# An FNO tokenizer with a transformer layer on one core: other matrix products and another order of steps in passes two and three

## The chip, the cores and the metric

The kernel runs on one core of a Trainium2 chip. The core has a matrix engine (TensorE, PE in the profile; its weight loads are listed apart as PEld), a vector engine (DVE), a scalar engine (ACT), a general engine (POOL) and a queue engine (SP) that here does nothing but issue transfers. All transfers share the core's 16 DMA engines. The metric is the device time of one execution in microseconds.

## The reference, cut to what matters

A batch of 64 images of 256 x 256 points goes through four Fourier layers of 32 channels, whose result is joined with 77 rows of text per image and goes through one transformer layer (attention, then a feed-forward over a selected half of the tokens). The change lies in the Fourier layers:

```python
v = h @ p_w + p_b                                  # (B, 32, 256, 256)
for i in range(4):
    x_ft = rfft2(v)                                # only 24 x 12 modes are used
    out_ft = modes of x_ft times fw1[i], fw2[i]    # mixes the 32 channels
    v = irfft2(out_ft) + einsum('bcxy,cd->bdxy', v, w_w[i]) + w_b[i]
    v = (v - mean(v)) * rsqrt(var(v) + 1e-5) * bn_g[i] + bn_b[i]   # over batch and points
    if i < 3: v = relu(v)
out = einsum('bcxy,cu->bxyu', v, q_w) + q_b
```

The mean and variance of layer i+1 are taken over all images, so a whole pass over the batch must be done before the next layer can be normalised. For the variance the kernel needs, among other sums, the sum over all points of the square of `v @ w_w[i+1]`.

## The kernel before, in words

**Stages.** `forward_first` transforms the raw images (0 to 110 us). Then, for each layer, `mix` multiplies the modes by the layer's weights and works out the normalisation; and for layers 0, 1 and 2 `layer` makes one pass over the 64 images. These are the three passes. The first (about 190 to 2547 us) takes the raw image as its input; the second (2624 to 5560 us) and the third (5637 to 8530 us) load the image's values that the pass before has stored in DRAM. The transformer layer follows (8640 us to the end).

**One image in a pass** is cut into eight chunks t = 0 to 7 of 1 MB each: 128 partitions (four groups of 32 channels) by 8 rows of 256 values. All data is fp32; every matrix product is issued as two MATMULs. The steps of one image, as `layer` names them:

- `am` loads the image's modes into `ams` (two transfers on SP, then a scaling on POOL). `sp0`, `sp1` expand the modes along x for chunks 0 to 3 and 4 to 7 (L662, PE), and `spT0`, `spT1` turn the result around on DVE into `y0`, `y1` (L670).
- `ld` t loads a chunk of the layer's input into `vin` (L656, two transfers of 512 KB on SP). The first pass has none.
- `pre` t makes the layer's output for a chunk in PSUM: 8 products of the inverse transform along y (L682) and 16 products of the channel matrix on 32x32 tiles (L693). `evA` and `evB` apply the ReLU to the two halves and write them to `vo`, on ACT (`.a`, L705) or DVE (`.d`, L707), as the word says.
- `st` t stores the chunk for the next pass (L714, two transfers of 512 KB).
- `turn` t transposes 32x32 blocks of the chunk into `t32` on DVE (L719).
- `prod` t multiplies the chunk by the next layer's channel matrix, 16 products on 32x32 tiles (L730), and `sqA`, `sqB` square and sum the two halves on ACT (L741).
- `y0` to `y7` transform the whole image along y, 16 products each, all accumulating in the same PSUM tiles (L752); `half`, `zt0` and `zt1` take the result out (L762 on ACT, L770 on DVE).
- `x` transforms along x: for each of three groups of modes four products with the image as the stationary operand (128x128) and 96 columns of the table `FX` as the moving one (L786). `xo` copies the result out on ACT (L797) and `xs` sends it to DRAM (L803).

**What sets the order.** The order is written out by hand: a pass repeats the list of words of `ORDER` once per image (the first entry for the first pass, the second for the second and third). `word@k` does the step for the image k further on, so several images are under way at once. Each engine takes its steps strictly in this order; steps on different engines meet only through semaphores. SP, too, issues transfers in the order of the list, and a transfer that waits holds up those behind it. In the program each transfer on SP also waits for the one eight before it to have landed.

**Buffers.** PSUM is a ring of four tiles of two banks (`take` gives a step the tiles that were freed first, `close` frees one); `pre`, `prod` and `y` take two, `sp` and `x` one. The y steps hold two tiles from y0 until `half` and `zt0`. `vin` and `vo` have four buffers each, `t32` six (a buffer holds two chunks). A `vo` buffer is free again when its chunk has been stored, turned and multiplied. Which chunk follows which in a buffer comes from the order in which they become free: in the second and third pass evA3 and evB3 write the buffer that the latest st6 stores, evA0 that of st5, evA7 that of st4, evA1 that of st2.

Of the kernel before, what the change touches and what calls it, by code (L numbers as in the profile page):

```python
# [9 lines left out]
F32 = mybir.dt.float32  # L10
# [7 lines left out]
C = 32  # L18
M = 12
KX = 2 * M  # L20
# [14 lines left out]
def _tables():  # L35
# [92 lines left out]
ORDER = [(  # L128
# [7 lines left out]
), (  # L136
# [7 lines left out]
)]  # L144

_TABLES, _GRIDS = _tables()
# [7 lines left out]
def tile_fno_fusion_transformer(ctx: ExitStack, tc: tile.TileContext, a, cst_d, grid_d, out):  # L154
    nc = tc.nc
    x = a["x"].rearrange("b x y o -> b x (y o)")
# [3 lines left out]
    const = ctx.enter_context(tc.tile_pool(name="const", bufs=1))  # L160
# [15 lines left out]
    T4, ID, ONES, CHAN = tab("t4"), tab("ident"), tab("ones"), tab("chan")  # L176

    CROW = tab("crow").rearrange("p (n k) -> p n k", n=4)

    epsc = const.tile([128, 1], F32, name="epsc")  # L180
    nc.vector.memset(epsc, EPS)

# [29 lines left out]
    w4 = [w4all[:, i, :] for i in range(L)]  # L212
# [333 lines left out]
    def layer(i, st, src, dst, acc):  # L546
# [3 lines left out]
        EX, FX = EXL[lay], FXL[lay]  # L550
# [3 lines left out]
        with ExitStack() as cx:  # L554
            def pool(name, bufs, **kw):
# [3 lines left out]
            op, yp, cp, xp, zp, tp = (  # L559
                pool(n, k, reuse_waits="tile")  # L560
                for n, k in (("lo", 4), ("ly", 1), ("lc", 1), ("lx", 2), ("lz", 1), ("lt", 6))
            )
# [20 lines left out]
            for n in range(nr):  # L583
# [4 lines left out]
                if n:  # L588
                    nc.vector.tensor_add(a0, a0, a1)
            nc.vector.tensor_copy(ams[1], ams[0])  # L590
            ws = cp.tile([128, C], F32, name="ws")
            if i:
                nc.vector.tensor_mul(ws, w4[i], s_)
            if i == 0:
                mv = [ip.tile([128, 4, 4 * S + 8], F32, name="mv") for n in range(2)]
                mv = [t[:, :, 0:4 * S].rearrange("p q (s y) -> p q s y", s=4) for t in mv]
                for t in mv:
                    nc.sync.dma_start(t, grid_d.rearrange("p (q s y) -> p q s y", q=4, s=4))

            ring, free, clock = {}, [0] * 4, [0]  # L600

            def take(key, n):

                clock[0] += 1
                mine = sorted((k for k in range(4) if free[k] >= 0), key=lambda k: free[k])[:n]
                for k in mine:
                    free[k] = -1
                ring[key] = [(k, pp.tile([128, 2, 512], F32, name=f"ring{k}")) for k in mine]
                return [t for _, t in ring[key]]

            def banks(key):
                return [t[:, n] for _, t in ring[key] for n in range(2)]
# [6 lines left out]
            y_, t32, vin, vo, half_, zts = {}, {}, {}, {}, {}, {}  # L619
# [104 lines left out]
            def prod(b, t, e):  # L724
                take(("prod", b, t), 2)
                ps = banks(("prod", b, t))
                for k in range(4):
                    for n in range(4):
                        j = (n + k) % 4
                        nc.tensor.matmul(  # L730
                            ps[n][32 * j:32 * j + 32], lhsT=w4[i + 1][32 * n:32 * n + 32],
                            rhs=vo[b, t][32 * n:32 * n + 32, 2 * j:2 * j + 2, :], start=True, stop=True,
                            skip_group_check=True, tile_position=(32 * n, 32 * j),
                        )

            def sq(n):
                def run(b, t, e):
                    key = "prod", b, t
                    at = 2 * (8 * b + t) + n
                    ps = ring[key][n][1]  # L740
                    nc.scalar.activation(ps, ps, AF.Square, accum_out=acc[:, at:at + 1])  # L741
                    close(key, n)
                return run
# [21 lines left out]
            def zt(h):  # L765
                def run(b, n, e):
                    if b not in zts:
                        zts[b] = zp.tile([128, 2, 32, C], F32, name="zt")
                    whole = h == 0 or b not in half_
                    nc.vector.transpose(  # L770
                        zts[b][:, h].rearrange("p k c -> p c k"),
                        (ring["y", b][h][1] if whole else half_[b]).rearrange("p n (s c) -> p c (n s)", c=C),
                    )
                    if whole:
                        close(("y", b), h)
                return run

            def x_(b, n, e):
                zt_ = zts.pop(b)
                ps = take(("x", b), 1)[0]  # L780
                for g in range(3):
                    n = 0
                    for h in range(2):
                        for r in range(2):
                            k0 = M * r + 4 * g
                            nc.tensor.matmul(  # L786
                                ps[:, 0, 96 * g:96 * g + 96],
                                lhsT=zt_[:, h, k0:k0 + 4, :].rearrange("p k c -> p (k c)"),
                                rhs=FX[:, h, 48 * r:48 * r + 96], start=n == 0, stop=n == 3,
                            )  # L790
                            n += 1

            xos = {}

            def xo(b, n, e):
                xos[b] = xp.tile([128, 3, 2 * KX], F32, name="xo")
                nc.scalar.copy(  # L797
                    xos[b], ring["x", b][0][1][:, 0, 0:288].rearrange("p (g k) -> p g k", g=3)[:, :, 0:2 * KX]
                )
                close(("x", b), 0)  # L800

            def xs(b, n, e):
# [1 line left out]

            run = dict(
                am=am, lx=lx, ld=ld, sp=sp, spT=spT, pre=pre, evA=ev(0), evB=ev(1), st=st_, turn=turn,
                prod=prod, sqA=sq(0), sqB=sq(1), y=y, half=half, zt0=zt(0), zt1=zt(1), x=x_, xo=xo, xs=xs,
            )
            steps = []
            for word in ORDER[min(i, 1)].split():  # L810
                word, _, late = word.partition("@")
                word, _, e = word.partition(".")
# [100 lines left out]
    with tc.tile_pool(name="tw", bufs=1) as tp, tc.tile_pool(name="tq", bufs=2, space=PSUM) as tq:  # L913
# [5 lines left out]
        for dh in range(2):  # L919
            ps = tq.tile([128, D], F32, name="wtp")  # L920
# [313 lines left out]
```

## Time and profile before

| | |
|---|---|
| median of 5 runs | 11277.61 us (11274.02 to 11296.37) |
| the profiled execution | 11296.37 us, span 11294.6 us |
| mean granted clock of TensorE | 0.984 of full speed |
| second pass, 2624 to 5560 us | PE busy 2796.64, DVE 2182.48, ACT 1747.69 us; DMA share 0.98 |
| third pass, 5637 to 8530 us | PE busy 2759.01, DVE 2159.55, ACT 1729.01 us; DMA share 0.98 |
| transfers of chunks (all three passes) | 3072 stores and 2048 loads of 512 KB |
| median time from issue to landing, 2700 to 5500 us | stores 8.8 us, loads 9.1 us |

The profile lists instructions by source line (L693 is line 693 of the kernel before), with what is written and read by the program's names. A group's row gives the number of instructions, the busy time, the mean duration and the idle time of the engine before them with what ended it. Matmuls overlap and their ends are modelled, so that a busy PE need not be a full PE. The DMA share is the time of all packets over 16 engines; since packets overlap a little, it can read over 1. The profiled execution was the slowest of the five.

### The profile page before, as it was taken

To read this page: it belongs to the slowest core of one execution; us is meant where nothing else is said; L and a number is where in the kernel's file an instruction comes from. 1 tells how busy PE (TensorE), PEld (TensorE's weight loads), DVE (VectorE), ACT (ScalarE), POOL (GpSimd) and SP (SyncE) were. 2 spreads that over 40 slices of the span, in tenths; PEclk is the share of its full clock that TensorE was granted. 3 is DMA by queue.
4 is the path that set the end of the run, shared out by engine and by line. 5 is a ranking of instruction groups with operands and counts; after the bars stand their busy time and mean duration, and the time that the engine had idled before them with its cause. 6 is when DMAs were issued, how large, how long until landed. Compare 5 with 4: busy or idle time off the path is not lost.

```text
span 11294.6 us, 409300 instructions
## 1 busy us (share of the span) xinstructions
PE 10611.1 (94%) x182550; PEld 5729.7 (51%) x182550; DVE 8448.3 (75%) x10381; ACT 6472.7 (57%) x10673; POOL 1446.2 (13%) x2179
## 2 busy tenths in 40 slices
PE   6999999998999999999799999999996999999999
PEld 3555555554444444444444444444443666666666
DVE  6888888887777777777677777777775766666665
ACT  5777777775566655666565666556563333333333
POOL 1111111110000000000000000000000333333333
PEclk8999999998999999999899999999998999999999
DMA  6766676678999999999899999999998555555553
GB/s 212 248 246 247 249 247 247 245 254 316 382 381 383 380 377 377 375 379 378 303 378 381 377 377 380 380 373 377 372 378 296 226 227 227 226 227 227 226 227 138
DMA packets 972545, 3457.31 MB, mean 306 GB/s; under 512 B 149784, under 2 KB 199320, under 8 KB 903832
## 3 DMA queue, kind: packets, MB, share of 16 engines
q1 hardware_dynamic: 905344, 3366.80, 77.8%
q0 software_dynamic: 58288, 60.60, 2.3%
q8 instruction: 1429, 23.41, 0.8%
q10 hardware_dynamic: 7144, 3.72, 0.1%
q14 instruction: 340, 2.79, 0.1%
HBM read 1733.60 MB, written 1696.92 MB: 304 GB/s over the span
## 4 chain that ended last, share of the span: by engine, by line
PE 61%; DMA 21%; DVE 9%; ACT 3%; issue 3%; SPq 2%; POOL 0%; ACTq 0%; DVEq 0%; POOLq 0%
PE ring L752 15%; DMA v<-vo 12%; PE ring L682 9%; PE ring L730 8%; DMA vin<-v 6%; PE ring L693 5%; PE hp L982 3%; PE ring L662 3%; PE pp L1145 3%; PE pp L1156 3%; PE ring L786 2%; DVE vo L707 2%; PE pp L1110 2%; DMA xh<-xo 2%; PE pp L1175 2%
## 5 line engine op out<-in xcount | busy, mean ns | idle before, releaser
L741 ACT ACTIVATE ring<-ring 128x1024 f32<-128x1024 f32 x3072 | 3115.8, 1014 | 1184.3 <-PE ring L730 1121.3
L719 DVE STREAM_TRANSPOSE t<-vo 128x2048 f32<-128x2048 f32 x1536 | 3465.7, 2286 | 21.4 <-DVE vo L707 0.9
L730 PE MATMUL ring<-vo,w 32*32 32x512 f32 x49152 | 2408.1, 600 | 85.0 <-ACT vo L705 69.0
L707 DVE TENSOR_SCALAR vo<-ring 128x1024 f32<-128x1024 f32 x1280 | 1544.7, 1221 | 1192.8 <-PE ring L693 799.1
L705 ACT ACTIVATE vo<-ring 128x1024 f32<-128x1024 f32 x1792 | 1792.3, 1023 | 1038.3 <-PE ring L693 484.7
L752 PE MATMUL ring<-t,cst 32*32 32x512 f32 x49152 | 2075.0, 599 | 53.8 <-issue 47.8
L752 PEld LDWEIGHTS ring<-t,cst 32*32 32x32 f32 x49152 | 909.7, 103 | 935.8 <-issue 635.6
L730 PEld LDWEIGHTS ring<-vo,w 32*32 32x32 f32 x49152 | 802.8, 103 | 1072.0 <-issue 401.5
L682 PE MATMUL ring<-cst,y 24*128 24x256 f32 x16384 | 1229.1, 402 | 77.6 <-DVE vo L707 60.1
L631 POOL TENSOR_TENSOR ams<-ams,bns 48x512 f32<-48x512 f32 x384 | 401.0, 1044 | 6991.5 <-DMA ams<-mix 6720.7
L693 PE MATMUL ring<-vin,ws 32*32 32x512 f32 x32768 | 1276.9, 603 | 18.0 <-issue 13.1
L682 PEld LDWEIGHTS ring<-cst,y 24*128 24x128 f32 x16384 | 789.3, 185 | 991.1 <-DVE vo L707 390.3
L670 DVE STREAM_TRANSPOSE y<-ring 128x1024 f32<-128x1024 f32 x384 | 763.3, 1988 | 329.4 <-PE ring L662 328.3
L682 PE MATMUL ring<-mv,y 29*128 29x256 f32 x8192 | 703.2, 404 | 36.5 <-ACT ring L741 20.1
L682 PEld LDWEIGHTS ring<-mv,y 29*128 29x128 f32 x8192 | 455.2, 185 | 368.9 <-ACT ring L741 210.3
L786 PEld LDWEIGHTS ring<-cst,zt 128*128 128x128 f32 x4608 | 531.9, 192 | 177.2 <-ACT vo L705 114.5
L762 ACT COPY half<-ring 128x1024 f32<-128x1024 f32 x192 | 194.4, 1013 | 737.9 <-PE ring L752 737.8
L1183 POOL DMA_DIRECT2D out_dram<-o x1024 | 510.7, 507 | 661.2 <-DVE o L1178 618.1
L741 ACT ACTIVATION_READ_ACCUMULATOR ring<-ring 128x1 f32 x3072 | 585.3, 191 | 0.0
L786 PE MATMUL ring<-cst,zt 128*128 128x96 f32 x4608 | 563.8, 279 | 6.3 <-DVE zt L770 5.3
L770 DVE STREAM_TRANSPOSE zt<-ring 128x1024 f32<-128x1024 f32 x192 | 377.4, 1965 | 249.7 <-PE ring L752 249.7
L662 PE MATMUL ring<-ams,cst 49*128 49x512 f32 (+1 forms) x1536 | 450.7, 642 | 105.2 <-POOL ams L631 36.7
(374 smaller groups left out, 9757.9 us busy)
## 6 DMA issues: line engine op xcount, KB each, us to landing
v<-vo SPq DMA_DIRECT2D x3072, 512.0 KB, 7.9
vin<-v SPq DMA_DIRECT2D x2048, 512.0 KB, 9.0
ch<-v SPq DMA_DIRECT2D x512, 1024.0 KB, 12.5
mix<-ob SPq DMA_DIRECT2D x96, 512.0 KB, 5.8
ams<-mix SPq DMA_DIRECT2D x384, 96.0 KB, 7.9
xin<-in_x_dram SPq DMA_DIRECT2D x16, 1024.0 KB, 6.0
mv<-in_x_dram POOLq DMA_DIRECT2D x256, 64.0 KB, 7.5
out_dram<-o POOLq DMA_DIRECT2D x1024, 16.0 KB, 3.0
```

The costliest lines, as they stand in the source:

```text
L662: nc.tensor.matmul(ps[:, n, :], lhsT=EX[hv, 128 * h:128 * h + 128], rhs=ams[b % 2][hv], start=True, stop=True, skip_group_check=True,)
L670: nc.vector.transpose(y_[b, h].rearrange("p q c -> p c q"), ring[key][0][1].rearrange("p n (c k) -> p (n c) k", k=32),)
L682: nc.tensor.matmul(ps[n][:, 256 * r:256 * r + 256], lhsT=y_[b, t // 4][32 * n:32 * n + K, q:q + 4, :].rearrange("p q c -> p (q c)"), rhs=m ...
L693: nc.tensor.matmul(ps[n][32 * j:32 * j + 32], lhsT=ws[32 * n:32 * n + 32], rhs=v[32 * n:32 * n + 32, 2 * j:2 * j + 2, :], start=False, sto ...
L705: nc.scalar.activation(to, ring[key][h][1], AF.Relu)
L707: nc.vector.tensor_scalar(to, ring[key][h][1], 0.0, None, ALU.max)
L719: nc.vector.transpose(t32[b, t // 2][:, :, 8 * (t % 2):8 * (t % 2) + 8, :].rearrange("p y s c -> p s y c"), vo[b, t].rearrange("p s (y l) ...
L730: nc.tensor.matmul(ps[n][32 * j:32 * j + 32], lhsT=w4[i + 1][32 * n:32 * n + 32], rhs=vo[b, t][32 * n:32 * n + 32, 2 * j:2 * j + 2, :], st ...
L741: nc.scalar.activation(ps, ps, AF.Square, accum_out=acc[:, at:at + 1])
L752: nc.tensor.matmul(ps[n][32 * j:32 * j + 32], lhsT=FYT[32 * n:32 * n + 32, k, :], rhs=t32[b, j][32 * n:32 * n + 32, k].rearrange("p s c -> ...
L786: nc.tensor.matmul(ps[:, 0, 96 * g:96 * g + 96], lhsT=zt_[:, h, k0:k0 + 4, :].rearrange("p k c -> p (k c)"), rhs=FX[:, h, 48 * r:48 * r + ...
L1183: nc.gpsimd.dma_start(out[b, 64 * n + 16 * g:64 * n + 16 * g + 16].rearrange("(p t) d -> p t d", t=2), o[32 * g + 8 * n:32 * g + 8 * n + 8 ...
```

## The change

Line numbers of the changed kernel are some 9 to 40 higher. Three things change in the second and third pass, and nothing in the first pass's order:

- **x transform.** The stationary operand is now the table: for each of two parts r and two halves h of the image's lines one product of 64 table columns (128x64) with 384 columns of the image as the moving operand, the two halves writing different halves of the partitions. The result lies the other way round, so `xe` copies it to SBUF (here on DVE) and `xt` makes three products with it as the stationary operand (128x128) and a doubled identity `ID2` of 48 columns as the moving one, which adds the two halves and turns them. These are seven products instead of twelve, and two new steps. `xo` reads the other bank.
- **Products for the squares.** For the words `prod1.w` and `prod7.w` the 16 products on 32x32 tiles become 8 products on 64x64 tiles, with the channel matrix twice on the diagonal of a 64x64 matrix (`w64`, made once per pass).
- **Order.** The second list of `ORDER` is another one. Among other things pre6 now stands between y1 and y2, pre2 of the image two further on stands after prod7 at the end, and st7, st0 and st6 of their images are issued among the y steps. The buffers follow each other differently too: evA7 and evB7 now write the buffer that st4 stores, evA0 that of st2, evA1 that of st5, evA6 that of st3, evA4 that of st1, evA5 that of st7, evA3 that of st6 and evA2 that of st0.

```diff
@@ ORDER, second list
-    "pre5 sqB7@-1 zt1@-1 sqA7@-1 pre6 evA5.a ld2@1 st4 evB5.d st5 turn4 evA6.a prod5 x@-1 "
-    "evB6.a sqB5 prod6 sqA5 xo@-1 turn5 pre2@1 sqA6 turn6 sqB6 prod4 evA2.a@1 evB2.d@1 "
-    "sqB4 ld0@1 ld7 sqA4 pre0@1 evB0.d@1 ld3@1 prod2@1 st6 evA0.a@1 turn2@1 sqB2@1 sqA2@1 "
-    "pre3@1 ld1@1 evA3.a@1 st2@1 evB3.d@1 pre7 evB7.d prod3@1 ld5@1 evA7.a sqA3@1 turn7 "
-    "pre1@1 st0@1 am@2 sqB3@1 prod0@1 evA1.a@1 evB1.d@1 sqA0@1 st7 sp1@1 st1@1 ld4@1 y0 "
-    "spT1@1 y1 ld6@1 turn0@1 turn3@1 xs@-2 y2 sqB0@1 prod1@1 y3 sqB1@1 sp0@2 y4 sqA1@1 "
-    "spT0@2 y5 y6 st3@1 turn1@1 y7 half.a pre4@1 zt0 prod7 evB4.d@1 evA4.a@1 "
+    "evB2.a@1 ld5 ld7 pre4 ld0@1 turn6 evA2.a@1 prod6 evA4.a x@-1 evB4.d xe.d@-1 turn4 "
+    "sqB6 prod4 xt@-1 st2@1 sqA6 turn2@1 sqA4 pre5 xo@-1 sqB4 am@2 evA5.d evB5.a pre3@1 "
+    "prod2@1 evA3.d@1 turn5 evB3.a@1 st4 xs@-1 sqA2@1 pre7 sqB2@1 evA7.a prod5 evB7.d "
+    "sqB5 pre0@1 st5 ld1@1 sqA5 prod3@1 turn7 evB0.a@1 sp1@1 sqA3@1 evA0.d@1 pre1@1 "
+    "sqB3@1 spT1@1 evA1.a@1 prod0@1 sqA0@1 ld6@1 evB1.d@1 ld2@2 st3@1 sp0@2 spT0@2 y0 "
+    "ld4@1 y1 st1@1 sqB0@1 turn3@1 turn0@1 pre6@1 y2 y3 evA6.a@1 y4 evB6.a@1 prod1.w@1 "
+    "sqB1@1 st7 sqA1@1 y5 st0@1 y6 st6@1 turn1@1 y7 prod7.w half.a zt0 sqA7 sqB7 ld3@2 "
+    "zt1 pre2@2 "
...
+    ID2 = const.tile([128, 2 * KX], F32, name="id2")
+    nc.vector.tensor_add(ID2, ID[:, 0:2 * KX], ID[:, 64:64 + 2 * KX])
...
+            w64 = cp.tile([128, 2, C], F32, name="w64")
+            nc.vector.memset(w64, 0.0)
+            for n in range(4):
+                nc.vector.tensor_copy(w64[32 * n:32 * n + 32, n % 2, :], w4[i + 1][32 * n:32 * n + 32])
+            w64 = w64.rearrange("p n o -> p (n o)")
...
@@ def prod(b, t, e)
+                if e == "w":
+                    for j in range(4):
+                        for n in range(2):
+                            m = (n + j) % 2
+                            nc.tensor.matmul(
+                                ps[j][64 * m:64 * m + 64], lhsT=w64[64 * n:64 * n + 64],
+                                rhs=vo[b, t][64 * n:64 * n + 64, 2 * j:2 * j + 2, :], start=True, stop=True,
+                                skip_group_check=True,
+                            )
+                    return
...
@@ def x_(b, n, e)
+                if turned:
+                    for r in range(2):
+                        for h in range(2):
+                            nc.tensor.matmul(
+                                ps[64 * h:64 * h + 64, 0, 0:384], lhsT=FX[:, h, 48 * r:48 * r + 64],
+                                rhs=zt_[:, h, M * r:M * r + M, :].rearrange("p k c -> p (k c)"),
+                                start=r == 0, stop=r == 1, skip_group_check=True,
+                            )
+                    return
...
+            def xe(b, n, e):
+                xes[b] = xp.tile([128, 384], F32, name="xe")
...
+                    nc.vector.tensor_copy(xes[b], ring["x", b][0][1][:, 0, 0:384])
+
+            def xt(b, n, e):
+                xe_ = xes.pop(b)
+                for g in range(3):
+                    nc.tensor.matmul(
+                        ring["x", b][0][1][:, 1, 96 * g:96 * g + 2 * KX],
+                        lhsT=xe_[:, 128 * g:128 * g + 128], rhs=ID2, start=True, stop=True,
+                    )
```

More of the change, by code (lines that the diff above doesn't have):

```diff
@@ L598, in layer @@
                     nc.sync.dma_start(t, grid_d.rearrange("p (q s y) -> p q s y", q=4, s=4))
+            turned = "xt" in ORDER[min(i, 1)]
             ring, free, clock = {}, [0] * 4, [0]
@@ L791, in x_ @@
                             n += 1
-            xos = {}
+            xos, xes = {}, {}
+            def xe(b, n, e):
+                xes[b] = xp.tile([128, 384], F32, name="xe")
+                if e == "a":
+                    nc.scalar.copy(xes[b], ring["x", b][0][1][:, 0, 0:384])
+                else:
+                    nc.vector.tensor_copy(xes[b], ring["x", b][0][1][:, 0, 0:384])
[6 more added lines that the diff above has]
+                    )
             def xo(b, n, e):
@@ L797, in xo @@
                 nc.scalar.copy(
-                    xos[b], ring["x", b][0][1][:, 0, 0:288].rearrange("p (g k) -> p g k", g=3)[:, :, 0:2 * KX]
+                    xos[b], ring["x", b][0][1][:, int(turned), 0:288].rearrange("p (g k) -> p g k", g=3)[:, :, 0:2 * KX]
                 )
@@ L806, in layer @@
                 am=am, lx=lx, ld=ld, sp=sp, spT=spT, pre=pre, evA=ev(0), evB=ev(1), st=st_, turn=turn,
-                prod=prod, sqA=sq(0), sqB=sq(1), y=y, half=half, zt0=zt(0), zt1=zt(1), x=x_, xo=xo, xs=xs,
+                prod=prod, sqA=sq(0), sqB=sq(1), y=y, half=half, zt0=zt(0), zt1=zt(1), x=x_, xe=xe,
+                xt=xt, xo=xo, xs=xs,
             )
```

## The prediction

> **What bounds the kernel now.** I read the page first (which stages are long and what is full in them), then the two passes that the change touches as windows, then the list of waits inside one of them, then one image instruction by instruction.
>
> The page's slices show the change's ground: the second and third passes are the two long stretches at 375 to 383 GB/s, with a DMA share of 9 tenths throughout, while PE reads 9 tenths everywhere.
>
> ```profile
> span 11294.6 us, 409300 instructions
> PE 10611.1 (94%) x182550; PEld 5729.7 (51%) x182550; DVE 8448.3 (75%) x10381; ACT 6472.7 (57%) x10673; POOL 1446.2 (13%) x2179
> DMA  6766676678999999999899999999998555555553
> ```
>
> The two passes as windows (columns: length, then busy time of PE, PEld, DVE, ACT, POOL, granted clock, DMA share, GB/s):
>
> ```profile
> 2624.00:5560.00 2936.00, 2796.64 (x59411) 1325.44 (x59420) 2182.48 (x1221) 1747.69 (x2752) 138.31 (x137) 0.99 0.98 376
> 5637.00:8530.00 2893.00, 2759.01 (x58643) 1296.64 (x58645) 2159.55 (x1205) 1729.01 (x2723) 133.81 (x128) 0.99 0.98 377
> ```
>
> Two resources look full, PE at 95% and DMA at 98%. Neither really is: of PE's busy time much is modelled tails, and DMA has dry spots. One image takes 45.4 us (2936/64 is 45.9, with the pass's two ends). Shorter windows inside one image:
>
> ```profile
> 4018.00:4020.00 2.00, 2.00 (x65) 0.85 (x67) 2.00 (x2) 0.79 (x2) 0.00 (x0) 1.00 0.75 297
> 4044.00:4058.00 14.00, 13.19 (x322) 6.52 (x307) 11.01 (x6) 3.64 (x7) 2.09 (x2) 1.00 1.03 413
> 4060.00:4062.00 2.00, 1.74 (x44) 1.04 (x48) 2.00 (x2) 1.89 (x4) 0.00 (x0) 1.00 0.80 317
> 4064.00:4066.00 2.00, 2.00 (x64) 0.60 (x32) 2.00 (x2) 1.07 (x2) 0.00 (x0) 1.00 0.69 270
> ```
>
> A full DMA reads 1.02 to 1.03, and once per image, just after the eight y steps, it falls to 0.7 or 0.8. So DMA alone would allow 45.4 x 0.98/1.02 = 43.6 us an image. SP's queue shows why it runs dry:
>
> ```profile
> 4007.37 1.52 SPq L656 DMA_DIRECT2D vin<-v  x2
> 4014.76 5.29 SPq L714 DMA_DIRECT2D v<-vo  x4
> ...
> 4023.72 1.07 SPq L714 DMA_DIRECT2D v<-vo  x2
> ```
>
> From 4008.9 to 4014.8 SP issues nothing: st4 waits for the evictions of pre4, which PE only reaches after y7. The bill comes twelve microseconds later, in the waits of 2700 to 5500 us (62 images):
>
> ```profile
> ACT vo L705 <- DMA v<-vo: 135.8, 92, 3.4
> DVE vo L707 <- DMA v<-vo: 132.8, 93, 3.4
> ```
>
> Both engines stand still together, 135.8/62 = 2.2 us an image, before evA3 and evB3: their vo buffer is still being stored by st6, which SP issued at 4023.72, late, and which frees them only at 4036.15 (row below), 12.4 us on. That is the one DMA wait of size.
>
> Last, the rows for the new operations, of the image at 4000 us and of the first transform at 40 us:
>
> ```profile
> 4020.72 2.92 PE L786 MATMUL ring<-cst,zt 128*128 128x96 f32 x24
> 4023.57 1.14 PE L730 MATMUL ring<-vo,w 32*32 32x512 f32 x32
> 4036.15 1.94 ACT L705 ACTIVATE vo<-ring 128x1024 f32<-128x1024 f32 x2 [1.99 <-DMA v<-vo]
> ```
> ```profile
> 45.11 1.94 PE L239 MATMUL ups<-xin,cst 128*64 128x512 f32 x8
> ```
>
> Every product is two MATMULs. x takes 4023.57 - 4020.72 = 2.85 us. L730's 32 MATMULs hold 16 tiles at once and stream in two rounds of 0.43 us. L239, on 128*64 tiles, holds two tiles: its 8 MATMULs are four rounds, (1.94 - 0.64)/3 = 0.43 us apart.
>
> **The change, part by part** (128 images in two passes; all else stands).
>
> *x transform.* Out: 24 MATMULs, 2.85 us. In: 8 MATMULs of L239's shape with 384 columns instead of 512, four rounds of 0.43 x 384/512 = 0.32, 1.3 us; then 6 of L786's pitch (2.85/24 = 0.12), 0.7 us; and two entries into another tile shape at some 0.2 (PE's step from L693 to L730, same shape, starts 0.3 after the last MATMUL; into L682 it takes 0.5). Sum 2.4 us: -0.45. Bounds: -1.3 (both parts fully hidden behind prod4's stream) and +0.5 (the 8 not paired: 2.6 + 0.7). The copy xe is 384 columns on DVE: between L797's 0.28 (144 columns) and L707's 1.22 (1024), I take 0.55. It waits for x, and behind it on DVE stand turn4, turn2 and evA5.d; prod2 waits for evA5. That is in the walk below.
>
> *Two products on 64x64 tiles.* 16 MATMULs, four tiles at once, four rounds of 0.43: 1.7 us against 0.86. With the shape changes I take 1.9 against 0.95, twice: +1.9 us an image, all in or right after the y stretch, where PE is alone on the path. Bounds for one: -0.45 (16 MATMULs at L457's 25 ns, 128 in 3.2 us) and +2.6 (the 16 one after the other at 0.21, 3.4 us). I take the value between, since L239's rounds fit it. The Trainium skill (TensorEngine Tiling, Gotcha 1: PSUM Pressure) says that different row tiles cannot use one PSUM bank at the same time; every tiled product in this trace gives each row group its own bank, while the new one lets both row groups write the same bank in different halves. If that made them take turns, the sum would be by the upper bound, +5.1 us an image; no row here shows it.
>
> *Order.* I walk through one image from the end of y7 with PE's prices (pre 1.97, prod 0.95, y 1.1, sp 1.07), ACT 1.02 an eviction and 1.2 a square, DVE 1.22, 2.0 (spT, zt) and 2.28 (turn), 0.25 from one engine to the next, ring tiles and no DMA wait.
> Before: pre4 0, prod7 2.5 (zt0), pre5 3.7, pre6 5.9 (sqA7), prod5 7.9, x 9.4, prod6 12.2, pre2 13.3, prod4 15.9 (sqB6), pre0 17.0, prod2 19.6, pre3 20.7, pre7 23.2, prod3 25.1, pre1 26.7, prod0 28.9, sp1 30.0, y0 31.4, prod1 34.7, sp0 37.2, end of y7 42.7. The image takes 45.4; the 2.7 left over are the 2.2 of DMA wait and 0.5 of small stalls.
> After: prod7.w 0, pre2 2.5 (zt0), pre4 4.5, prod6 6.9 (evA2), x 8.0, prod4 9.5, xt 10.6, pre5 11.4, pre3 13.6, prod2 16.3 (evA5.d behind turn4 and turn2), pre7 17.5, prod5 20.0 (sqB2), pre0 21.2, prod3 23.7 (sqA5), sp1 24.8, pre1 26.2 (sqA3), prod0 28.3, sp0 29.7, y0 30.9, pre6 33.3 (spT0), y2 35.2, prod1.w 38.5, y5 40.4, end of y7 43.7.
> So the engines' own chain grows by 1.0: -0.45 and +1.9 from the two edits, -0.45 from fewer ring waits.
>
> *Transfers in the new order.* A load or store of one chunk is 2.65 us of full DMA. What SP is given now: ld7 4.5, ld0 6.5, st2 6.8, (am) st4 8.2, (xs) st5 16.3, ld1 and ld6 16.3, ld2 and st3 19.5, ld4 23.2, st1, st7, st0 29.7, st6, ld3, ld5 37.5, then ld7 again. st7 and st0 are held back until the y stretch, so the longest pause (29.7 to 37.5) is met with three stores just queued. With a backlog of 2.5 us before st6 the DMA never runs dry; up to some 5 us, every buffer is back in time. The tightest pair is st4 and evA7, which takes its buffer: 8.2 to 19.9, 11.7 us. The same count for the old order wants at least 4.4 us for no dry spot and at most 5 for st6 to land before evA3 (10.2 to 23): no room with SP's issues of 0.4 to 0.8 us each, and the trace has both the dry spot and the wait. So I let 1.8 of the 2.2 us go, and 0.4 stay, at st4 or ld1. Bounds: all 2.2 stays, or all goes.
>
> *Once a pass:* w64's memset and four copies on DVE, 0.2 to 0.4 us each (L590's copy of 512 columns: 0.43), 2 us a pass at most, before a start that waits for the first ams anyway. The new order leads by the same two images; I put the ends at 0, within 10 us.
>
> Sum per image: +1.0 - 1.8 = -0.8 us; 128 x 0.8 = 102 us. Against the profiled execution (11296.37, span 11294.6 and 1.8 around it): 11194. That execution was the slowest of the five, 19 above the median 11277.61; for a median: **11176 us**, 0.9% faster.
>
> **Rivals.**
> *PE becomes the bound and the waits stay (slower).* The y stretch grows to y0 30.9 through prod7.w 45.6 with a pre inside; if st4 lands late before evA7, the wait has only moved. It costs +1.0 with the 2.2 kept: +128 us, 11405. It decides once more than 1.2 of the 2.2 us stay. For it: PE has 95%, and both full resources leave little room (43.7 walked, 43.6 DMA). Against: the list of pauses above.
> *The sixteen MATMULs go one after the other (slower by far):* +5.1 - 1.9 - 0.8 = +2.4 us, 11585.
> *DMA is the only bound:* PE's extra 1.9 us hides in stalls (PE shows 46 us of idle "issue" in 62 images, and the new form issues half the MATMULs), and the image falls to 43.6: -1.8 x 128 = -230, 11048.
> *No change:* the wait and the added PE time cancel, 11278 within 0.2% (23 us, about what a measurement of this kernel can tell).
>
> **How the numbers follow.** Forecast (20 to 190 us less) 0.44; DMA the only bound 0.14; no change 0.08; PE bound with the waits kept 0.28; one after the other 0.06. Faster 0.58, same 0.08, slower 0.34. The likeliest case's own range is 11090 to 11255. For 8 in 10 it must reach nearly to the DMA floor (11048) and to the kept waits (11405): 11060 to 11405, which leaves out the serial case and the far ends.
>
> **What would show it.** Right: waits of ACT and DVE for v<-vo under 0.6 us an image, no 2 us stretch under 0.85 DMA share, x's eight MATMULs 1.3 us, prod.w's sixteen 1.7 us, an image at 44.6. Wrong: evA7 or pre1's products idle on a transfer for 2 us; sixteen MATMULs over 3 us; DVE's evA5 idle-free behind turn2 with prod2 waiting more than 1 us; PE idle at pre6 for spT0.

## The result, and the profile after

The changed kernel takes 11291.62 us (median of 25 runs, 11271.85 to 11301.82) against 11285.33 us of the kernel before (45 runs): a ratio of 1.0005, 95% interval 1.0000 to 1.001. That is no change, where I had forecast 11176. The profiled execution has a span of 11289.5 us. The page of the changed kernel, first its span, then the busy time of each engine, then the DMA share in 40 slices:

```profile
span 11289.5 us, 398452 instructions
PE 10683.2 (95%) x177174; PEld 5518.4 (49%) x177174; DVE 8340.5 (74%) x10397; ACT 6594.5 (58%) x10801; POOL 1446.5 (13%) x2179
DMA  6676667678999999999899999999998555555553
```

There are 5376 MATMULs fewer than before, and PE is still busy for 72 us more. The two passes as windows (same columns as in the prediction) are as long as they were:

```profile
2624.00:5560.00 2936.00, 2839.54 (x56766) 1214.68 (x56766) 2126.05 (x1221) 1808.00 (x2816) 134.13 (x133) 0.99 0.98 376
5637.00:8530.00 2893.00, 2786.45 (x56037) 1196.12 (x56040) 2104.23 (x1203) 1789.70 (x2785) 130.13 (x125) 0.99 0.98 377
```

The list of waits of the changed kernel, 2700 to 5500 us, for the wait that I said would go (total us, times, longest):

```profile
ACT vo L714 <- DMA v<-vo: 69.5, 53, 3.8
DVE vo L716 <- DMA v<-vo: 68.2, 57, 3.6
```

It was halved, from 2.2 to 1.1 us an image (69.5/62), and yet the image did not get shorter: 45.3 us before and 45.4 after, from one `half` to the next, as the mean of images 6 to 57 of the second pass. (Means "per image" below are of those images, or a window's total over 62.) The new operations, and the eviction that now waits, in the timeline of one image of the changed kernel (start, duration, operation):

```profile
4008.46 1.95 PE L740 MATMUL ring<-vo,w 64*64 64x512 f32 x16
4022.01 1.51 PE L803 MATMUL ring<-zt,cst 128*64 128x384 f32 x8
4023.57 0.56 DVE L828 COPY xe<-ring 128x384 f32<-128x384 f32 x1 [1.35 <-PE ring L803]
4024.52 0.87 PE L833 MATMUL ring<-id,xe 128*128 128x48 f32 x6
4034.53 1.02 ACT L714 ACTIVATE vo<-ring 128x1024 f32<-128x1024 f32 x1 [0.85 <-DMA v<-vo]
```

The last line is evA7, waiting for st4. SP's issues show how st4 came to be late (start, duration, operation):

```profile
4009.55 12.24 SPq L665 DMA_DIRECT2D vin<-v  x6
4021.88 0.87 SPq L723 DMA_DIRECT2D v<-vo  x2
4022.84 0.91 SPq L632 DMA_DIRECT2D ams<-mix  x2
4023.84 1.42 SPq L723 DMA_DIRECT2D v<-vo  x2
```

The first line holds ld5, then ld7 and ld0, which only end at 4021.79; st2, am and st4 stand behind them. And the DMA still runs dry once an image, soon after the y steps, as it did before (a window of two us, 4 us after that image's `half`; length, busy times, granted clock, DMA share, GB/s):

```profile
4064.00:4066.00 2.00, 2.00 (x64) 1.10 (x49) 1.91 (x1) 1.65 (x2) 0.00 (x0) 1.00 0.52 137
```

### The profile page after: what moved, and what is told of

It is laid out like the page before. It is cut to its first block, busy times and chain, and to the rows that moved or that the text cites. A ratio compares the mean times of both kernels' runs of the same rounds, so it can differ in the third digit from the quotient of the medians.

```text
span 11289.5 us, 398452 instructions
## 1 busy us (share of the span) xinstructions
PE 10683.2 (95%) x177174; PEld 5518.4 (49%) x177174; DVE 8340.5 (74%) x10397; ACT 6594.5 (58%) x10801; POOL 1446.5 (13%) x2179
## 3 DMA queue, kind: packets, MB, share of 16 engines
q8 instruction: 1386, 22.71, 0.8%
## 4 chain that ended last, share of the span: by engine, by line
PE 67%; DMA 15%; DVE 8%; ACT 5%; issue 2%; SPq 2%; POOL 0%; ACTq 0%; DVEq 0%; POOLq 0%
PE ring L771 16%; PE ring L691 11%; DMA v<-vo 10%; PE ring L702 7%; PE ring L749 6%; PE ring L740 4%; PE hp L1026 3%; PE ring L671 3%; ACT vo L714 3%; PE pp L1189 3%; PE pp L1200 3%; PE pp L1154 2%; DMA xh<-xo 2%; PE pp L1219 2%; PE pp L1116 1%
## 5 line engine op out<-in xcount | busy, mean ns | idle before, releaser
L714 ACT ACTIVATE vo<-ring 128x1024 f32<-128x1024 f32 x1920 | 1917.7, 1023 | 1680.7 <-PE ring L702 1274.0
L771 PE MATMUL ring<-t,cst 32*32 32x512 f32 x49152 | 2002.9, 599 | 19.7 <-issue 14.7
L749 PE MATMUL ring<-vo,w 32*32 32x512 f32 x40960 | 1895.1, 603 | 25.6 <-ACT vo L714 24.0
L716 DVE TENSOR_SCALAR vo<-ring 128x1024 f32<-128x1024 f32 x1152 | 1391.9, 1217 | 531.2 <-PE ring L702 264.4
L691 PE MATMUL ring<-cst,y 24*128 24x256 f32 x16384 | 1309.0, 404 | 158.8 <-ACT vo L714 125.8
L771 PEld LDWEIGHTS ring<-t,cst 32*32 32x32 f32 x49152 | 852.8, 103 | 966.9 <-issue 608.3
L702 PE MATMUL ring<-vin,ws 32*32 32x512 f32 x32768 | 1203.8, 607 | 3.1 <-issue 1.6
L749 PEld LDWEIGHTS ring<-vo,w 32*32 32x32 f32 x40960 | 647.7, 103 | 846.5 <-issue 414.3
L740 PE MATMUL ring<-vo,w 64*64 64x512 f32 x4096 | 504.3, 602 | 0.5 <-issue 0.4
L1026 PE MATMUL hp<-ch,win 128*32 128x512 f32 x4096 | 470.4, 599 | 10.1 <-DMA ch<-v 9.8
L702 PEld LDWEIGHTS ring<-vin,ws 32*32 32x32 f32 x32768 | 248.1, 103 | 356.6 <-issue 224.1
```

Of the source, the lines that this page charges most:

```text
L691: nc.tensor.matmul(ps[n][:, 256 * r:256 * r + 256], lhsT=y_[b, t // 4][32 * n:32 * n + K, q:q + 4, :].rearrange("p q c -> p (q c)"), rhs=m ...
L702: nc.tensor.matmul(ps[n][32 * j:32 * j + 32], lhsT=ws[32 * n:32 * n + 32], rhs=v[32 * n:32 * n + 32, 2 * j:2 * j + 2, :], start=False, sto ...
L714: nc.scalar.activation(to, ring[key][h][1], AF.Relu)
L716: nc.vector.tensor_scalar(to, ring[key][h][1], 0.0, None, ALU.max)
L740: nc.tensor.matmul(ps[j][64 * m:64 * m + 64], lhsT=w64[64 * n:64 * n + 64], rhs=vo[b, t][64 * n:64 * n + 64, 2 * j:2 * j + 2, :], start=Tr ...
L749: nc.tensor.matmul(ps[n][32 * j:32 * j + 32], lhsT=w4[i + 1][32 * n:32 * n + 32], rhs=vo[b, t][32 * n:32 * n + 32, 2 * j:2 * j + 2, :], st ...
```

## The experiments

"Before" and "after" are the two kernels of the change; a ratio is against runs of the kernel before that were taken along with it.

### The parts of the change, each alone

My first theory was the prediction's own: the 64x64 products cost 1.9 us an image on the engines' path, and ate the gain.

**After without the 64x64 products.**

```diff
-    ... evB6.a@1 prod1.w@1 ... y7 prod7.w half.a ...
+    ... evB6.a@1 prod1@1 ... y7 prod7 half.a ...
```

> The changed kernel with prod1 and prod7 on 32x32 tiles again, all else as changed. Theory 1 (the 64x64 products lie on the engines' own chain and eat what the order saves): the sixteen MATMULs of each take 1.9 us against 0.95, and leaving them out gives 1.9 us an image back, down to the DMA's 43.6 at most: 1.5 to 1.8 us x 128, 190 to 230 us less than the changed kernel, 11060 to 11100. Rival 2 (the transfers set the image in either order, the wait for st4 before evA7 has only taken the place of the one for st6): PE's time in the y stretch is hidden, within 30 us of the changed kernel.

Measured: 11403.06 us, ratio 1.0107 (1.0092 to 1.0123). The kernel became slower by 112 us. The theory falls: taking away the operation that streams longest costs time. Rival 2, which allowed 30 us, falls with it. The same run is also the new order with the new x transform alone: without the 64x64 products these two, from which the gain was to come, make the kernel before 1.1% slower. The granted clock of the profiled execution is lower too, 0.978 against 0.982 in the changed kernel; even if all time went by that clock, it would be 0.4%, about 46 us (an estimate), and not the 112.

**Before with the 64x64 products.**

```diff
-    ... y2 sqB0@1 prod1@1 y3 ... zt0 prod7 evB4.d@1 ...
+    ... y2 sqB0@1 prod1.w@1 y3 ... zt0 prod7.w evB4.d@1 ...
```

> The kernel before, in its old order and with its old x transform, with prod1 and prod7 alone on 64x64 tiles. Theory 1: +1.9 us an image on the y stretch, which is also the stretch that runs the DMA dry there: +200 to +260 us. Rival 2: hidden beside the transfers, less than +60 us. A third reading (half as many MATMULs are fetched and issued, so the stalls marked issue shrink): 0 or less.

Measured: 11283.02 us, ratio 1.0000 (0.9991 to 1.0009). In the old order they cost nothing and bring nothing, within what rival 2 and the third reading allowed.

In the new order the list of waits names what came in their place. Here are the lines of PE without a releaser ("issue"), 2700 to 5500 us; first the changed kernel, then the one without 64x64 products:

```profile
PE ring L771 <- issue: 6.2, 14, 0.8
```
```profile
PE ring L771 <- issue: 78.6, 61, 2.0
PE ring L749 <- issue: 31.0, 26, 1.9
```

In the middle of the y steps (L771) PE stands still for up to 2 us and waits for nothing that the profile shows. What comes just ahead of the end of such a stall is in the trace too. All 151 stalls of over 1 us between two instructions of one line (2700 to 5500 us; 42 in before, 11 in after, 71 in the kernel without 64x64 products, 27 in the one with half the streaming time below) end 1.15 to 1.75 us after a packet on the queue of kind "instruction" has landed; of random moments 9 in 100 would lie there. In the other eleven kernels of this case the same holds for all 167 stalls of this length for which the profile names no releaser. The page counts those packets (packets, MB, share), here of the changed kernel and then of the one without 64x64 products:

```profile
q8 instruction: 1386, 22.71, 0.8%
```
```profile
PE 10571.0 (93%) x181270; PEld 5606.5 (49%) x181270; DVE 8338.1 (73%) x10397; ACT 6592.9 (58%) x10801; POOL 1442.8 (13%) x2179
q8 instruction: 1418, 23.23, 0.8%
```

2 x 177174 / 1386 = 255.7 and 2 x 181270 / 1418 = 255.7: one packet for 256 of PE's MATMULs and weight loads. A y step is 64 of these in 1.11 us, so that four y steps use up a packet in 4.4 us. I count as fetch stalls all of over 0.5 us that end in that distance from a packet. They are 1.1 us an image in before, 0.4 in after, 2.5 without the 64x64 products, and 0.2 in before with them. Without the 64x64 products the stalls thus grow by 2.1 us an image. The streaming saved is 0.95 us if prod1 alone lies on PE's path, and 1.9 if prod7, which stands beside zt0, does too; that leaves +0.2 to +1.15, and 0.9 (112/128) was measured.

**Before with the new x transform** (xe behind evB6, xt ahead of xo).

```diff
-    ... evB6.a sqB5 ... sqA5 xo@-1 turn5 ...
+    ... evB6.a xe.d@-1 sqB5 ... sqA5 xt@-1 xo@-1 turn5 ...
```

> The kernel before, in its old order, with the new x transform alone: xe.d before sqB5, xt before xo. Theory 1: PE's chain runs through x there (x 9.4, prod6 12.2), so 2.85 - 1.5 us come free at prod6, and 0.85 for xt goes in after it: -0.45 us an image, -60 us, and up to -130 if pre2 gains the whole. Rival 2: within 25 us of before.

Measured: 11288.45 us, ratio 1.0003 (0.9993 to 1.0013); nothing, as rival 2 had it. The wait for st6 is still there, 131.6/62 = 2.1 us an image; x stands ahead of evA3 that waits for it.

**After with the old x transform.**

```diff
-    ... evB4.d xe.d@-1 turn4 sqB6 prod4 xt@-1 st2@1 ...
+    ... evB4.d turn4 sqB6 prod4 st2@1 ...
```

> The changed kernel with the old x transform of twelve products (xe and xt left out of the order). Theory 1: x takes 2.85 instead of 1.5 at the head of the image and xt's 0.85 goes: +0.5 us an image, +60 us. But DVE loses xe (0.56 us) ahead of turn4, turn2 and evA5, for which prod2 waits: 0 to +60. Rival 2: within 25 us of the changed kernel.

Measured: 11358.63 us, ratio 1.0068 (1.0053 to 1.0083). In the new order the new x is worth 67 us, 0.5 an image, close to the 0.45 of the prediction; in the old order, just above, it was worth nothing.

### Streaming time or the number of instructions

**After with two products of half the streaming time.** It has as many instructions as after.

```diff
@@ prod, e == "w"
-    for j in range(4):
-        for n in range(2):
-            m = (n + j) % 2
-            nc.tensor.matmul(ps[j][64 * m:64 * m + 64], lhsT=w64[64 * n:64 * n + 64],
-                rhs=vo[b, t][64 * n:64 * n + 64, 2 * j:2 * j + 2, :], ...)
+    for m in range(2):
+        for n in range(4):
+            j = (n + m) % 4
+            nc.tensor.matmul(ps[n][64 * m:64 * m + 64], lhsT=w64[32 * n:32 * n + 32],
+                rhs=vo[b, t][32 * n:32 * n + 32, 2 * j:2 * j + 2, :],
+                tile_position=(32 * n, 64 * m), ...)
```

> The changed kernel, but prod1.w and prod7.w are 8 products on 32x64 tiles (8 tiles at once) instead of 8 on 64x64 tiles (4 at once): as many instructions, and half the time to stream. It leaves out half of the computation: each of these products reads one group of 32 channels for two quarters of the result, so the sums of squares are not the reference's. Theory 1 (the 64x64 products' streaming time is on the engines' path): one of the two, prod1.w, stands inside the y stretch and gives its 0.95 us back, prod7.w stands beside zt0 and gives nothing; 128 x 0.95 = 120 us, about 11170. Fetch theory (PE in the y stretch is held by the arrival of its instructions, 256 to a packet, and the longer streaming only fills time in which it would stand): most of it comes back as stalls of PE without a releaser; 11230 to 11290.

Measured: 11279.04 us, ratio 0.9991 (0.9981 to 1.0). The products take 1.04 to 1.2 us instead of 1.88 until PE's next instruction, and the kernel gains 12 us of the 120 that the streaming time would give. Its list of waits:

```profile
PE ring L771 <- issue: 21.8, 36, 1.1
ACT vo L714 <- DMA v<-vo: 84.4, 56, 3.6
```

The fetch stalls went from 0.4 to 0.9 us an image, and the wait for st4 from 1.1 to 1.4. Against the kernel without 64x64 products, which streams about as long (0.95 us by the prediction's price) but has 64 instructions more per image, it is 124 us faster, 1.0 an image, with 1.6 us less of fetch stalls. So it is the number of instructions in the y stretch that counts here, and the longer stream of the 64x64 products fills time in which PE would stand.

### Transfers or engines

**Before with a quarter of the transfers left out**: the second store of each chunk in passes two and three is not made.

```diff
@@ st_
-    for n in range(2):
+    for n in range(1 if i else 2):
@@
-    layer(i, st, vd[(i + 1) % 2], vd[i % 2], acc)
+    layer(i, st, vd[0], vd[min(i, 1)], acc)
```

> The kernel before, but in the second and third pass only the first of a chunk's two stores is made, and the third pass and the last layer load what the first pass stored: a quarter of the transfers is left out, and the values loaded are not the reference's. No engine's instructions change. If the engines' own chain is 45.4 less the 2.2 us of DMA wait, an image takes 43.2: 11285 - 128 x 2.2 = about 11005 us. If waits for transfers only hid the fetch stalls of PE (1.1 us an image), these grow and the gain is 1.1 or less: 11145 or more.

Measured: 11151.17 us, ratio 0.9877 (0.9858 to 0.9897): 134 us, 1.05 an image, where I had put the wait at 2.2. The second branch of the expectation (1.1 or less, 11145 or more) has the number but not the reason: the fetch stalls did not grow, they stay at 1.1 us an image. The edit lightens the transfers as a whole, so it bounds what all waits for them cost and does not single one out. The waits of ACT and DVE for st6 are gone altogether. But the same two engines then wait for PE's pre in their place. The lists of before and of this kernel:

```profile
DVE vo L707 <- PE ring L693: 381.2, 261, 3.4
ACT vo L705 <- PE ring L693: 208.3, 198, 2.9
```
```profile
DVE vo L707 <- PE ring L693: 444.7, 381, 4.2
ACT vo L705 <- PE ring L693: 321.1, 357, 2.9
```

Of ACT's 135.8 us of DMA wait, 112.8 came back as a wait for pre, and of DVE's 132.8, 63.5. Step by step: evA3 goes 1.85 us earlier (23.5 instead of 25.4 after `half`), evA7 only 0.7 earlier, since its pre7 is not done sooner; it had been idle for 0.1 us ahead of evA7 and is now idle for 1.2.

**After with the same left out.**

```diff
-    for n in range(2):
+    for n in range(1 if i else 2):
@@
-    layer(i, st, vd[(i + 1) % 2], vd[i % 2], acc)
+    layer(i, st, vd[0], vd[min(i, 1)], acc)
```

> The changed kernel with the same left out (the second of a chunk's two stores in the second and third pass; later loads read what the first pass stored). The engines' chain of the new order without DMA waits should be 45.4 - 1.1 = 44.3 us an image: about 11150 us, so some 140 us more than the order of before with the same left out. If it comes out as fast as that or faster, the engines' chain did not grow, and my walk of it is wrong.

Measured: 11100.39 us, ratio 0.9832 (0.9813 to 0.9852): 1.5 an image under after (191/128), 50 us under the 11150 expected, and faster than the old order with the same left out. Here nothing takes the wait's place; the list of after and of this kernel:

```profile
ACT vo L714 <- PE ring L702: 594.4, 438, 4.9
```
```profile
ACT vo L714 <- PE ring L702: 604.8, 489, 4.4
```

The images take 44.3 us in the old order and 43.9 in the new one. So without the press of transfers the change does gain 0.4 us, and with it this is given back: transfers cost the old order 1.0 an image and the new one 1.5.

**After without 64x64 products, with the same left out**: the edit just shown, and

```diff
-    ... evB6.a@1 prod1.w@1 ... y7 prod7.w half.a ...
+    ... evB6.a@1 prod1@1 ... y7 prod7 half.a ...
```

> The changed kernel with prod1 and prod7 on 32x32 tiles (32 MATMULs each, as before the change) and with a quarter of the transfers left out (the second of a chunk's two stores in the second and third pass; later loads read what the first pass stored), so that waits for transfers can't blur it. Engines' chain by streaming time alone: prod1's 0.95 us is saved, 43.9 - 0.95 = 43.0 us an image, 11100 - 120 = about 10980. Fetch theory: 64 more instructions in the y stretch bring back some 2.2 us of stalls an image, 43.9 - 0.95 + 2.2 = 45.2: about 11260 us, with the stalls inside the y steps at 2.5 us an image as in the run with all transfers.

Measured: 11056.49 us, ratio 0.9803 (0.9783 to 0.9823), faster than the kernel above by 44 us (two executions of each, and the two intervals overlap between 0.981 and 0.982). Neither expectation holds. The fetch stalls are there, but 1.2 us an image instead of the 2.5 with all transfers; with the 64x64 products they are 0.2 instead of 0.4. So the 64x64 products cost 0.35 an image (44/128) when transfers are light, and gain 0.9 (112/128) when DMA is full. Of the 1.25 us between, the stalls that they save account for 1.1 (2.1 against 1.0): the price of PE's instructions hangs on the load of the DMA engines.

### Mending the wait

**After with st4 ahead of st2 and am.**

```diff
-    ... prod4 xt@-1 st2@1 sqA6 ... sqB4 am@2 evA5.d ... evB3.a@1 st4 xs@-1 ...
+    ... prod4 xt@-1 st4 st2@1 sqA6 ... sqB4 evA5.d ... evB3.a@1 am@2 xs@-1 ...
```

> The changed kernel with st4 issued right after xt, ahead of st2, instead of behind ld0, st2 and am; am@2 takes st4's old place. Theory (the 1.1 us for which evA7 and evB7 wait per image until st4 has landed is what cancelled the gain; nothing else keeps the engines): the wait goes, and no other comes; an image takes 45.4 - 1.1 = 44.3 us, 11290 - 128 x 1.1 = about 11150 us. Rival (there is too little room between the engines' chain, 44.3, and the transfers, 43.6 plus a dry spot, for one moved store to help; the wait moves on, to st2 and evA0 or to a load): within 40 us of the changed kernel, 11250 to 11330, with the same idle time before other evictions or before a pre.

Measured: 11232.88 us, ratio 0.9949 (0.9933 to 0.9966), about 60 us less than after, between the theory's 11150 and the rival's 11250. evA7 no longer waits, and its step stands 0.9 earlier. More than half of that is lost again: evA1, behind pre1, which now waits for ld1, stands only 0.4 earlier, and evA6 only 0.2. The list books another 80 us to st3 ahead of evA6, 1.3 an image, but it puts a whole idle stretch down to what ended it: ACT is idle there for 3.9 us, and for 3.7 in after, so that st3 adds only 0.2.

**The same, with ld2@2 in the y stretch.**

```diff
-    ... evB1.d@1 ld2@2 st3@1 sp0@2 ... y1 st1@1 sqB0@1 ...
+    ... evB1.d@1 st3@1 sp0@2 ... y1 st1@1 ld2@2 sqB0@1 ...
```

> The changed kernel with st4 moved as in the run before, and ld2@2 issued behind st1@1 in the y stretch instead of ahead of st3: it landed at 33 us and is read at 47.5, while st3, behind it, landed at 35.3 with evA6 due at 34.9. Theory (the transfers pass 43.4 us of work an image and cost time only where one lands after the engine needs it): evA6's wait of 1.45 us goes too, since st3 lands 2.65 us sooner; what is left is pre1 behind ld1. An image takes 44.0 to 44.4 us, 11290 - 128 x (1.0 to 1.4) = 11110 to 11160. Rival (the sum of transfers plus the dry spot sets the time, and a wait removed comes back elsewhere): 11210 to 11250, no better than the run with st4 alone.

Measured: 11274.35 us, ratio 0.9992 (0.9983 to 1.0002). The 80 us booked to st3 are gone, and the kernel is slower than the last by some 40 us: a miss for the theory, and for the rival too (11210 to 11250).

**The same, with ld1@1 ahead of st5.**

```diff
-    ... pre0@1 st5 ld1@1 sqA5 ...
+    ... pre0@1 ld1@1 st5 sqA5 ...
```

> The same, and ld1@1 ahead of st5 instead of behind it: ld1 lands 2.65 us sooner (24.5 for pre1 due at 26.2), st5 as much later (27.3 for evA1 due at 28.2). Theory: the last wait for a transfer goes and the engines' own chain, 43.9 us, is left: 11290 - 128 x 1.5 = about 11100 us, as with a quarter of the transfers left out (11100.39). Rival: as for the run before, 11210 to 11250; or evA1 now waits for st5, and it is as slow as the run with st5 ahead.

Measured: 11195.64 us, ratio 0.9926 (0.9911 to 0.9941). Faster than the rival allowed (11210), but not the 11100 of the theory.

**After with st4 and ld1 moved, ld2@2 left in place**, and **the same with st3 ahead of ld2@2**.

```diff
-    ... prod4 xt@-1 st2@1 sqA6 ... sqB4 am@2 evA5.d ... evB3.a@1 st4 xs@-1 ...
-    ... pre0@1 st5 ld1@1 sqA5 ...
+    ... prod4 xt@-1 st4 st2@1 sqA6 ... sqB4 evA5.d ... evB3.a@1 am@2 xs@-1 ...
+    ... pre0@1 ld1@1 st5 sqA5 ...
@@ the second also
-    ... evB1.d@1 ld2@2 st3@1 sp0@2 ...
+    ... evB1.d@1 st3@1 ld2@2 sp0@2 ...
```

> The changed kernel with st4 behind xt and ld1@1 ahead of st5; ld2@2 stays where the change put it, ahead of st3. If pre1's wait for ld1 (evA1 idle 2.0 to 2.1 us instead of 1.4) set the time of the two runs before, it goes: 0.4 to 0.6 us an image under the run with st4 alone, 11233 - 128 x 0.5 = about 11170, with evA6 waiting some 1.4 us for st3. If a load in the y stretch is what hurts, it is also faster than the run with both (11196). If evA6's wait for st3 decides, it is slower than 11196.

> The same, and st3@1 directly ahead of ld2@2 instead of behind it, both still ahead of the y stretch. Every store and load then lands before it is needed by the landings seen (st3 about 32.7 for 34.9, ld2 about 35.3 for 47.5, ld1 25.4 for 26.2): if waits at evictions and at pre are all that transfers cost, an image takes 44.0, about 11110. If the y steps stay some 0.75 us longer than with a quarter of the transfers left out, 44.7 and 11195.

Measured: 11190.2 us, ratio 0.9922 (0.9907 to 0.9937), and 11192.8 us, ratio 0.9925 (0.9908 to 0.9941). The first is 20 us above the 11170 expected, the second at the 11195 of its second branch. Both are faster than the two kernels of the change, by 0.8%. Their lists of waits for stores, of the first and of the second:

```profile
ACT vo L714 <- DMA v<-vo: 237.5, 56, 5.5
DVE vo L716 <- DMA v<-vo: 8.1, 11, 1.1
```
```profile
ACT vo L714 <- DMA v<-vo: 35.3, 22, 4.1
DVE vo L716 <- DMA v<-vo: 14.4, 21, 1.2
```

One has 3.8 us of DMA wait an image on ACT and the other 0.6, and they take the same time. The list again books more than the store costs: ahead of evA6 ACT is idle for 4.7 us in the first, where mostly st3 ends it, and for 3.8 in the second, where pre6 does. So st3 holds evA6 back by 0.8 us (36.0 instead of 35.3 after `half`), and the chain does not pass through it. With transfers lined up this way, DMA is nearly full through the pass: 1.00, where the prediction's full stretches read 1.02 to 1.03 (the second pass of the first of the two):

```profile
2700.00:5500.00 2800.00, 2761.96 (x55576) 1189.82 (x55568) 2077.61 (x1189) 1773.55 (x2757) 131.88 (x131) 1.00 1.00 383
```

What is left against the kernel with a quarter of the transfers left out (44.6 and 43.9 us an image) lies in the y steps. y2 to y4 and y5 to y7 stand in runs of three, seen here in the timeline of the changed kernel:

```profile
4050.23 4.49 PE L771 MATMUL ring<-t,cst 32*32 32x512 f32 x96
4054.65 1.95 PE L740 MATMUL ring<-vo,w 64*64 64x512 f32 x16
4056.53 3.40 PE L771 MATMUL ring<-t,cst 32*32 32x512 f32 x96
4059.86 1.95 PE L740 MATMUL ring<-vo,w 64*64 64x512 f32 x16
```

Up to the next product the first run takes 4.42 and the second 3.33 us. A run's mean is 3.87 in after, 3.85 and 3.86 in these two, and 3.53 with the transfers left out: 2 x 0.32 = 0.65 us an image, nearly all of the difference. The fetch stalls over 0.5 us account for some 0.3 of it (0.5 against 0.2 us an image); the rest is spread over shorter gaps, and whether that too is the arrival of instructions stays open. So does why ld2@2 in the y stretch costs 40 us: the fetch stalls grew from 0.4 to 0.65 an image there, but pre1's wait for ld1 blurs the comparison, and with ld1 early the same place cost next to nothing (11196 against 11193).

## Why the prediction was wrong

Its sum was "+1.0 - 1.8 = -0.8 us" an image. The runs give -0.4 and +0.5, which is about the +0.1 (6 us over 128 images is 0.05) that was measured. Here -0.4 is the difference of the two orders with a quarter of the transfers left out, and +0.5 is what all transfers add more to the new order (1.5) than to the old (1.0). Both terms came out with the other sign, and their errors (-1.4 and +2.3) partly cancel: that the result lies about 1% from the forecast is luck.

**The step that failed: "So I let 1.8 of the 2.2 us go, and 0.4 stay, at st4 or ld1".** Two things are wrong in it.

First, its base. "The image takes 45.4; the 2.7 left over are the 2.2 of DMA wait and 0.5 of small stalls": the 2.2 us are idle time of ACT and DVE (1.9 of them before evA3, where I put them all, and 0.3 before evA1), and I took them for time of the image. With a quarter of the transfers left out, and no such wait, the old order is only 1.05 us faster. The walk itself could have told: pre3 at 20.7 and pre7 at 23.2 put evA3 at 22.9 and evA7 at 25.4 (1.97 and 0.25 later), so that between them ACT, with 1.02 for evA3, is idle for 1.5 us in any case, and a late evA3 uses these up first. The other 1.6 of the 2.7 are stalls, of which 1.1 are fetch stalls.

Second, what stays. The pair was named rightly ("st4 and evA7, which takes its buffer"), but 1.1 us of wait stayed instead of 0.4, and in the new order it costs nearly its full length (with the transfers lightened evA7 stands 0.9 us earlier). The rest of the 1.5 us that transfers cost the new order, some 0.6, lies in the slower y steps, for which the prediction had no term. I had st4 issued at 8.2 and the queue at "some 5 us" at most. On the mean it was issued at 10.0 and 10.75, and landed at 20.6, 9.8 us after the second issue, with evA7 ready at 19.5. SP is held by ld7 and ld0, and behind these stand st2, am and st4, in this order. The list of pauses had "the longest pause (29.7 to 37.5)" and missed that from ld5's second issue near 41.8 to ld7, which goes at 4.3 of the next image, SP issues nothing for 8 us: there the DMA runs dry, and then ld7, ld0, st2, am and st4 are asked for one upon the other.

**The engines' chain (+1.0).** Walked: 42.7 before and 43.7 after. With transfers light, 44.3 and 43.9. The new order's walk is right to 0.2; the old one's is short by 1.6, because of stalls for which the walk had no term. I had read the "issue" time of PE as slack in which the 64x64 products could hide (the rival in which DMA alone bounds); it is a cost of its own that these products remove. "+1.9 us an image, all in or right after the y stretch" was measured as the duration (1.88 against about 0.95), but not as a cost: 0.35 when transfers are light, and a gain of 0.9 when they are not.

**The x transform (-0.45)** held in the new order: 1.51 and 0.87 us in the timeline where 1.3 and 0.7 with two changes of shape were worked out, and 67 us, 0.5 an image, when it alone is undone. In the old order it brought nothing.

**The rivals.** "The sixteen MATMULs go one after the other" is excluded by the 1.88 us. Its price was also mis-sized: at the 0.43 us of a round, 3.4 us is two MATMULs at a time, and all sixteen one after the other would be 6.9. Here the Trainium skill (TensorEngine Tiling, Gotcha 1: PSUM Pressure) rules out two row tiles in one bank at the same time; the trace does not agree for tiles that write different partition halves of the bank: the sixteen MATMULs start in four groups of four, some 0.43 us apart, and with turns in each bank they would take 3.4 us. "No change: the wait and the added PE time cancel" is what came out as a time, but not for its reason: the added PE time is not there. The rival "PE becomes the bound and the waits stay" had the mechanism nearest to the truth, st4 late before evA7.

**What would show it.** Waits under 0.6 us: 1.1. No stretch under 0.85 DMA share: 0.52 at 4064. x's MATMULs 1.3 us: 1.51. prod.w 1.7 us: 1.88. An image at 44.6: 45.4 in after, and 44.6 in the kernel with st4 and ld1 moved. (Of the lines read at the start one was read wrongly, and nothing rests on it: the third pass's slices stand at 372 to 381 GB/s, not 375 to 383.)

## What to carry to other kernels

An engine's wait is not time of the loop until a walk with the wait put in, and the walk without it, end at different times: here 2.2 us of wait were worth 1.05, 1.1 us were worth almost all of it, and 3.8 us nothing. A list of waits also books a whole idle stretch to what ended it: of those 3.8 us the store made 0.8, and ACT would have stood for the rest in any case. Before a "no reason" idle of PE is booked as slack, look whether it ends at a fixed distance from the arrival of an instruction packet; if so, half as many MATMULs can be free or better, as here, although the product streams twice as long. In an order with a hand-written transfer queue, write down for each buffer when its store is issued, what is queued ahead of it then, and when it must have landed: moving three words (st4, am and ld1) gained 0.8%, where the whole change had gained nothing.

## What the runs showed of the hardware that was not expected

- PE's instructions arrive as packets on a DMA queue of their own: 16.4 KB each (22.71 MB / 1386), one for 256 MATMULs and weight loads. In four kernels all 151 stalls of over 1 us inside a line's instructions ended 1.15 to 1.75 us after such a packet had landed, and in the other eleven all 167 without a releaser.
- How long PE stands for them depends on the load of the transfers: without 64x64 products 2.5 us an image at a DMA share of 0.96, and 1.2 at 0.83. A packet's own time is the same in both (median 0.97 and 0.96 us), so it is not the packet itself that takes longer. That the packets wait behind data was not shown.
- Sixteen MATMULs on four 64x64 tiles, two of which share a bank in different partition halves, take 1.88 us to the next instruction (5th to 75th percentile 1.877), four rounds of 0.43 and a shape change; eight 32x64 tiles take 1.04 to 1.2.
